# The second feed-forward product of nine blocks as seven quadrant products, with the weight sums formed on chip

## The chip, the cores and the metric

The kernel runs on one core of one Trainium2 chip. The metric is the time of one execution on the device in microseconds (us). Before the change three runs took 1843.79 to 1845.49 us, with a median of 1844.52 us.

## The reference

Two layers of a graph transformer over 2708 nodes with 512 features. All arithmetic is f32. Each layer does this (the adjacency has about 9 neighbours in a row, so a node attends to few others):

```python
q, k, v = h @ Wq.T + bq, h @ Wk.T + bk, h @ Wv.T + bv      # 8 heads of 64
attn = softmax(where(mask == 0, -1e9, q @ k.T / 8))
h1 = layer_norm(h + attn @ v @ Wo.T + bo)
ff = relu(h1 @ W1.T + b1) @ W2.T + b2                      # 512 -> 2048 -> 512
h2 = layer_norm(h1 + ff)
```

The change is in the product with `W2`, in layer 0 alone.

## The kernel before, in words

The kernel turns the adjacency into a list of neighbours for each node, sorts the nodes by the length of their lists into 22 tiles of 128 nodes, and gathers only the listed rows of keys and values. It takes the tiles in 11 blocks of two tiles each (`blocks`, L1581); the last block has a tile of 20 nodes, so its two tiles make 148 columns instead of 256.

The order of the work is written by hand on every engine: each engine runs its instructions in the order in which the program emits them, and an engine that waits holds back all that stands behind it. The order comes from interleaved generators. For each block the main loop (L1753 to L1825) steps through `feed_forward` (L1447), which yields sixteen times, once for each chunk f of 128 of the 2048 hidden features. Between two yields the loop emits other work:

- **The feed-forward itself, on TensorE.** Step f does four matmuls `pf` (L1494) with `W1` as the stationary operand and the 256 columns of the two tiles moving. ScalarE applies the bias and relu and writes `ft` (L1505), 128 features by 256 nodes. Three steps later (`LAG`), `second` (L1460, matmul at L1467) multiplies: for each of the two tiles, `ft` of that tile is stationary, and a 128 by 512 piece of `W2` moves, into the accumulators `a0` and `a1`. After step 15 the last three steps of each tile follow, first of tile one, then of tile two.
- **The end of a block, on VectorE.** L1536 adds the accumulator to the residual; `norm` (L1253) does the layer norm, with a power on GpSimd (L1263) in its middle.
- **The attention of later blocks, on VectorE, ScalarE and GpSimd** (`attend`, L1586). Its steps handle one chunk of up to two neighbours for each node of a tile. VectorE multiplies keys by queries (L1136), sums over heads (L1142), and for the chunk of the step before weighs the values (L1168) and adds them up (L1175 or L1183). ScalarE does the exponentials (L1155) and the scaling of the second neighbour's values (L1162). GpSimd issues the gathers (L1099), three chunks ahead. `advance` (L1645) gives the attention a share of steps after each f, by the table `PACE` (L55): in layer 0 the share is 0.6 after f = 2 to 4, 1.2 after 5 to 8, 0.6 after 9 and 10, 0.8 after 13 to 15, and none after 0, 1, 11 and 12. The first block has its own table `PACES`.
- **The next layer's keys and values** (`keys_values`, L1544): at f = 5 the block before is transposed, at f = 6 and f = 7 its two tiles are multiplied by `Wk` and `Wv`, with VectorE reading the keys out of the accumulator (L1561) and ScalarE the values (L1564). At f = 8 GpSimd puts the rows into DRAM.
- **The next block's input** (`attended`, L1414): at f = 10 and 11 the attended rows are transposed, and at f = 11 multiplied by `Wo`; VectorE adds the residual and norms (L1429 on). At f = 15 the result is transposed again into `hT` (`turned`, L1438).

ps_a, ps_f and ps are the pools of accumulators (one bank of 2 KB a partition for each tile); before, ps_f and ps have three places each. While layer 0 attends, the gathered rows use five places of their own and the place of `Wq`, whose use in layer 0 is over (L1218). SP's queue carries stores and loads: in these blocks the stores of L1566 and L1567.

Of the kernel before, what the change touches and what calls it, by code (L numbers as in the profile page):

```python
# [8 lines left out]
F32 = mybir.dt.float32  # L9
# [14 lines left out]
NC = DM // P  # L24
NP = NH // 2
NFC = FF // P
# [14 lines left out]
KVB = 5  # L41
# [439 lines left out]
def by_edges(ctx: ExitStack, tc: tile.TileContext, x, xT, adj, layers, out, redo):  # L481
# [9 lines left out]
    nc = tc.nc  # L491
# [3 lines left out]
    NL = len(layers)  # L495
# [11 lines left out]
    dram = ctx.enter_context(tc.tile_pool(name="dram", bufs=1, space=DRAM))  # L507
# [5 lines left out]
    ps_f = ctx.enter_context(tc.tile_pool(name="ps_f", bufs=3, space=PSUM))  # L513
    ps = ctx.enter_context(tc.tile_pool(name="ps", bufs=3, space=PSUM))

    own = {}
    all_lines = []
    all_made = []
# [21 lines left out]
    q_d = [dram.tile([N, DM], F32, name=f"q_d{n}") for n in range(NL)]  # L540
    zT_d = [None] + [dram.tile([NT, P, NC, P], F32, name=f"zT_d{n}") for n in range(1, NL)]
    xb_d = [None] + [dram.tile([N, DM], F32, name=f"xb_d{n}") for n in range(1, NL)]
    rec_d = dram.tile([P * NT, 2 * LIST], F32, name="rec_d")

    def chunked(ap):
        return ap.rearrange("(c p) n -> p c n", p=P)
# [578 lines left out]
    class Tile:  # L1125
# [53 lines left out]
        def sums(self, peak):  # L1179
            r, g, S, acc, wide = self.r, self.g, CAPS[self.g], self.acc, self.wide  # L1180
            while wide > 1:
                h = wide // 2
                nc.vector.tensor_tensor(  # L1183
                    acc[:r, :h, :], acc[:r, :h, :], acc[:r, wide - h : wide, :], ALU.add
                )
                wide -= h
            nc.vector.tensor_reduce(
                peak[:r, g : g + 1],
                self.sc[:r, :S, :].rearrange("p s h -> p (s h)"),
                AX.X,  # L1190
                ALU.max,
                apply_absolute_value=True,
            )
# [20 lines left out]
    def rows_of_keys(n):  # L1214

        if n == NL - 1 and not places:
            places.extend([None] * KVB + ["wk", "wv"])
        elif n < NL - 1 and all_made and not places:  # L1218
            places.extend([None] * KVB + ["wq"])
        tag = places[0] if places else None  # L1220
        if places:
            places.append(places.pop(0))
        if tag is None:
            return at.tile([P, SLOTS, 2 * DM], F32, tag="kv", name="kv", bufs=KVB)
        kv = wts.tile([P, NC, DM], F32, tag=tag, name="kv")
        return kv.rearrange("p c n -> p (c n)").rearrange("p (s n) -> p s n", s=SLOTS)
# [55 lines left out]
    class Layer:  # L1282
# [164 lines left out]
        def feed_forward(self, block, hs, hT):  # L1447
# [93 lines left out]
                zs.append(z)  # L1541
            yield zs

        def keys_values(self, block, zs):  # L1544
# [160 lines left out]
    for n in range(NL):  # L1705
# [47 lines left out]
        for k, block in enumerate(blocks):  # L1753
# [5 lines left out]
            for f, zs in enumerate(now.feed_forward(block, hs, hT)):  # L1759
                if f == NFC:  # L1760
                    break
                if f in (5, 6, 7, 8) and behind:
# [19 lines left out]
                    now.load_w2(len(now.w2), nc.scalar)  # L1782
                if n > 0 and (k, f) == (0, 2):
                    now.load_second(1, temp)
                if last and not more and f == 8:
                    checked()
                if last and not more and f == 10:
# [104 lines left out]
```

## Time and profile before

| what | us |
|---|---|
| three runs, lowest, median, highest | 1843.79, 1844.52, 1845.49 |
| the profiled execution's own time | 1844.31 |
| its span | 1842.3 |
| TensorE busy in the span | 1827.5 (99%) |
| VectorE busy in the span | 1374.4 (75%) |
| the nine changed blocks, from the first `pf` of block 1 to the first `pf` of block 10 | 313.23 to 1016.53 |

The profile is of one execution. PE is TensorE's matmul stream, PEld its weight loads, DVE is VectorE, ACT is ScalarE, POOL is GpSimd, SP is SyncE. One matmul of the program in f32 shows as two records, so step f's four `pf` matmuls show as eight. A record's duration overlaps with the next one's. How long a stream takes is therefore read from where records start, not from their mean length.

### The profile page before, as it was taken

To read this page: it belongs to the slowest core of one execution; us is meant where nothing else is said; L and a number is where in the kernel's file an instruction comes from. 1 tells how busy PE (TensorE), PEld (TensorE's weight loads), DVE (VectorE), ACT (ScalarE), POOL (GpSimd) and SP (SyncE) were. 2 spreads that over 40 slices of the span, in tenths; PEclk is the share of its full clock that TensorE was granted. 3 is DMA by queue.
4 is the path that set the end of the run, shared out by engine and by line. 5 is a ranking of instruction groups with operands and counts; after the bars stand their busy time and mean duration, and the time that the engine had idled before them with its cause. 6 is when DMAs were issued, how large, how long until landed. Compare 5 with 4: busy or idle time off the path is not lost.

```text
span 1842.3 us, 20976 instructions
## 1 busy us (share of the span) xinstructions
PE 1827.5 (99%) x6195; PEld 1092.6 (59%) x6195; DVE 1374.4 (75%) x2147; ACT 945.0 (51%) x3263; POOL 782.2 (42%) x745
## 2 busy tenths in 40 slices
PE   9999999999999999999999999999999999999997
PEld 4444466565666656566565544666666666666666
DVE  4986778787777776767774157877998988898853
ACT  4770445554456545555543113655665675567531
POOL 3334755544435434443431032444563645455302
PEclk9999999999999999999999999999999999999999
DMA  9997987644546455553631676845564654555300
GB/s 339 377 340 257 372 273 243 226 158 165 204 139 234 144 187 183 177 182 105 223 121 46 229 264 250 299 132 205 177 225 147 245 206 177 183 197 207 118 12 21
DMA packets 129829, 368.01 MB, mean 200 GB/s; under 512 B 14378, under 2 KB 32670, under 8 KB 129704
## 3 DMA queue, kind: packets, MB, share of 16 engines
q0 software_dynamic: 70608, 252.12, 39.7%
q1 hardware_dynamic: 48938, 92.85, 14.1%
q10 hardware_dynamic: 10158, 21.61, 3.1%
q8 instruction: 50, 0.82, 0.2%
q14 instruction: 75, 0.61, 0.1%
HBM read 315.84 MB, written 50.68 MB: 199 GB/s over the span
## 4 chain that ended last, share of the span: by engine, by line
PE 93%; DVE 3%; ACT 1%; DMA 1%; issue 1%; POOL 0%; SPq 0%; ACTq 0%; POOLq 0%; DVEq 0%
PE pf L1494 30%; PE a L1467 29%; PE o L606 8%; PE v L606 8%; PE k L606 8%; PE q L606 8%; PE tp L1273 3%; DVE sc L1142 1%; DVE kv L1136 1%; ACT kv L1162 1%; PE a L1482 0%; DMA zT<-zT_d 0%; DMA w<-in_W 0%; DMA q<-q_d,ident_i 0%; ACT cx L1206 0%
## 5 line engine op out<-in xcount | busy, mean ns | idle before, releaser
L1494 PE MATMUL pf<-hT,w 128*128 128x256 f32 (+1 forms) x2816 | 631.3, 371 | 0.1
L1494 PEld LDWEIGHTS pf<-hT,w 128*128 128x128 f32 x2816 | 517.7, 190 | 172.6 <-issue 107.0
L1099 POOL DMA_INDIRECT kv<-kv_d,listed x420 | 506.9, 1207 | 253.1 <-issue 113.3
L1467 PE MATMUL a<-w,ft 128*128 128x512 f32 x1312 | 611.1, 592 | 0.0
L1505 ACT ACTIVATE ft<-pf,b 128x256 f32<-128x256 f32 (+1 forms) x336 | 153.9, 461 | 412.0 <-PE pf L1494 402.1
L1467 PEld LDWEIGHTS a<-w,ft 128*128 128x128 f32 x1312 | 246.8, 190 | 187.4 <-issue 165.9
L1263 POOL TENSOR_TENSOR rd<-va,mhalf 128x1 f32<-128x1 f32 (+1 forms) x88 | 81.2, 922 | 564.7 <-DVE va L1261 564.6
L1162 ACT ACTIVATE kv<-kv,p 128x64 f32<-128x64 f32 x1232 | 311.0, 334 | 5.0
L1136 DVE TENSOR_TENSOR kv<-kv,q 128x1024 f32<-128x1024 f32 (+1 forms) x222 | 256.8, 1157 | 14.9 <-DMA q<-q_d,ident_i 13.4
L1142 DVE TENSOR_REDUCE sc<-kv 128x16 f32<-128x1024 f32 (+1 forms) x222 | 257.9, 1162 | 7.6
L1175 DVE TENSOR_TENSOR acc<-acc,kv 128x1024 f32<-128x1024 f32 (+2 forms) x178 | 205.2, 1153 | 76.6 <-ACT kv L1162 60.5
L1155 ACT ACTIVATE p<-sc,listed 128x8 f32<-128x8 f32 x420 | 104.3, 299 | 123.1 <-DVE sc L1142 100.5
L1168 DVE TENSOR_TENSOR kv<-kv,p 128x512 f32<-128x512 f32 (+1 forms) x178 | 123.1, 691 | 36.2 <-ACT p L1155 31.1
L606 PE MATMUL o<-wo,cT 128*128 128x512 f32 x336 | 148.2, 594 | 0.6 <-ACT cT L1278 0.6
L606 PEld LDWEIGHTS o<-wo,cT 128*128 128x128 f32 x336 | 62.2, 190 | 72.5 <-issue 61.7
L731 DVE MAX8 tops<-code 128x8 f32<-128x247 f32 (+2 forms) x242 | 78.7, 399 | 27.1 <-ACT code L726 26.7
L1267 DVE SCALAR_TENSOR_TENSOR h<-h,rd,ln_b 128x512 f32<-128x512 f32 (+1 forms) x88 | 66.1, 751 | 41.0 <-POOL rd L1263 41.0
L1206 ACT ACTIVATE cx<-acc,su 128x64 f32<-128x64 f32 (+1 forms) x352 | 88.2, 332 | 12.9 <-DVE su L1198 7.5
L1162 ACT ACTIVATE acc<-kv,p 128x64 f32<-128x64 f32 (+1 forms) x352 | 88.8, 334 | 1.4
L726 ACT ACTIVATE code<-aj 128x1354 bf16<-128x1354 int32 (+1 forms) x44 | 73.6, 1723 | 21.9 <-POOL aj L720 18.2
L1564 ACT COPY kvs<-v 128x512 f32<-128x512 f32 (+1 forms) x22 | 12.9, 585 | 137.3 <-PE v L606 136.6
L1429 DVE TENSOR_TENSOR h<-o,xb 128x512 f32<-128x512 f32 (+1 forms) x44 | 30.2, 687 | 65.6 <-PE o L606 48.4
(183 smaller groups left out, 1601.7 us busy)
## 6 DMA issues: line engine op xcount, KB each, us to landing
aj<-in_adj SPq DMA_DIRECT2D x42, 677.0 KB
kv_d<-kvs ACTq DMA_DIRECT2D x21, 512.0 KB
xg<-in_xT SPq DMA_DIRECT2D x19, 512.0 KB
w<-in_W SPq DMA_DIRECT2D x16, 512.0 KB
kv<-kv_d,listed POOLq DMA_INDIRECT x420
zT_d<-zT SPq DMA_DIRECT2D x22, 256.0 KB
xb_d<-h SPq DMA_DIRECT2D x21, 256.0 KB
q<-q_d SPq DMA_DIRECT2D x21, 256.0 KB
```

The costliest lines, as they stand in the source:

```text
L606: nc.tensor.matmul(o[:r], xs(c), wm[:, c, :], start=(c == 0), stop=(c == NC - 1))
L1099: return nc.gpsimd.indirect_dma_start(out=to, out_offset=None, in_=table[:, :], in_offset=bass.IndirectOffsetOnAxis(ap=s, axis=0), bounds_ ...
L1136: nc.vector.tensor_tensor(kv[:r, :c, :DM], kv[:r, :c, :DM], self.q[:r].unsqueeze(1).to_broadcast([r, c, DM]), ALU.mult,)
L1142: nc.vector.tensor_reduce(self.sc[:r, s0 : s0 + c, :], kv[:r, :c, :DM].rearrange("p s (h d) -> p s h d", d=DK), AX.X, ALU.add,)
L1155: nc.scalar.activation(p[:r, s, :], self.sc[:r, s, :], AF.Exp, bias=minus[:r, g, s : s + 1])
L1162: nc.scalar.activation(to[:, i, hd], kv[:r, i, DM + h * DK : DM + (h + 1) * DK], AF.Copy, scale=p[:r, s0 + i, h : h + 1],)
L1168: nc.vector.tensor_tensor(to[:, 0, :].rearrange("p (h d) -> p h d", d=DK), kv[:r, 0, DM:].rearrange("p (h d) -> p h d", d=DK), p[:r, s0, : ...
L1175: nc.vector.tensor_tensor(self.acc[:r, :c, :], self.acc[:r, :c, :], kv[:r, :c, DM:], ALU.add)
L1206: nc.scalar.activation(cx[:r, hd], self.acc[:r, 0, hd], AF.Copy, scale=self.su[:r, h : h + 1])
L1467: nc.tensor.matmul(a[:r, cols], fts[f][:, c0 : c0 + r], self.w2[f // 2][:, f % 2, cols], start=(f == 0), stop=(f == NFC - 1),)
L1494: nc.tensor.matmul(pf[:, :w], self.w1[f // 2][:, c, f % 2 * P : f % 2 * P + P], hT[:, c, :w], start=(c == 0), stop=(c == NC - 1),)
L1505: nc.scalar.activation(ft[:, :w], pf[:, :w], AF.Relu, bias=self.b1[:, f : f + 1])
```

## The change

Blocks 1 to 9 of layer 0 (k = 1 to 9, both tiles full) no longer do four matmuls of 512 columns for each pair of chunks f = 2j and 2j + 1. For the first seven pairs they do seven matmuls of 256 columns each (`products`). The left operands are quadrants of the two `ft` tiles and three combinations of them, `s[0]` to `s[2]`; the right operands are quadrants of `W2` and three combinations of them, `t2` to `t4`. One quadrant of `W2` is overwritten by a difference. The eighth pair is done as before, with the second tile's matmuls split into halves.

- VectorE forms the left combinations: `sums` emits four operations of 128 by 128 for each pair. One of them overwrites the second half of an `ft` tile. They are emitted after step f = 2j + 2; the products follow at f = 2j + 3.
- The right combinations are formed by VectorE in block 0 (`form`, four operations of 128 by 256 for each of seven pairs, six of them at f = 5, 7, ... 15 and the seventh at the start of block 1), stored to DRAM on SP's queue, and read back for every pair of every block into five slots (`ask_forms`), three loads of 128 KB for a pair. The slots and the left combinations lie in the place of `Wq`, so the gathers have five places instead of six.
- There are two accumulators more (`c0`, `c1`). ps_f and ps have two places instead of three in blocks 1 to 9.
- At the end of a block nine operations on VectorE put the four accumulators together, in place of two.
- In block 9 the overwritten quadrants of `W2` are loaded again.

```diff
@@ rows_of_keys
-        elif n < NL - 1 and all_made and not places:
-            places.extend([None] * KVB + ["wq"])
@@ class Layer
+        def form(self, j):
+            w, W = self.w2[j], 2 * P
+            b11, b12, b21, b22 = w[:, 0, :W], w[:, 0, W:], w[:, 1, :W], w[:, 1, W:]
+            t2, t3, t4 = (self.slots[(3 * j + i) % 5] for i in range(3))
+            nc.vector.tensor_tensor(t3, b22, b12, ALU.subtract)
+            nc.vector.tensor_tensor(b12, b12, b11, ALU.subtract)
+            nc.vector.tensor_tensor(t2, b22, b12, ALU.subtract)
+            nc.vector.tensor_tensor(t4, b21, t2, ALU.subtract)
+            for i, t in enumerate((t2, t3, t4)):
+                nc.sync.dma_start(out=form_d[j, i], in_=t)
...
+        def ask_forms(self, upto):
+            while self.asked < upto:
+                n = self.asked
+                j, i = n // 3 % (NFC // 2 - 1), n % 3
+                nc.sync.dma_start(out=self.slots[n % 5], in_=form_d[j, i])
+                self.asked += 1
...
+        def feed_forward_by_seven(self, k, block, hs, hT):
...
+            def sums(j):
+                f0, f1 = fts[2 * j], fts[2 * j + 1]
+                s = self.sums[j % 2]
+                nc.vector.tensor_tensor(s[:, 0], f1[:, P:], f0[:, P:], ALU.add)
+                nc.vector.tensor_tensor(f0[:, P:], f0[:, :P], f0[:, P:], ALU.subtract)
+                nc.vector.tensor_tensor(s[:, 1], s[:, 0], f0[:, :P], ALU.subtract)
+                nc.vector.tensor_tensor(s[:, 2], f1[:, :P], s[:, 1], ALU.subtract)
+
+            def products(j):
+                f0, f1, w, s = fts[2 * j], fts[2 * j + 1], self.w2[j], self.sums[j % 2]
+                t2, t3, t4 = (self.slots[(base + 3 * j + i) % 5] for i in range(3))
+                first, last = j == 0, j == J - 1
+                for to, left, right, start, stop in (
+                    (c0[:, L], f0[:, :P], w[:, 0, L], first, False),
+                    (a0[:, L], f1[:, :P], w[:, 1, L], first, False),
+                    (a1[:, L], f1[:, P:], t4, first, False),
+                    (c0[:, R], s[:, 1], t2, False, last),
+                    (c1[:, L], f0[:, P:], t3, first, False),
+                    (c1[:, R], s[:, 0], w[:, 0, R], False, last),
+                    (a0[:, R], s[:, 2], w[:, 1, R], False, False),
+                ):
+                    nc.tensor.matmul(to, left, right, start=start, stop=stop)
...
+                if f % 2 == 0 and j > 0:
+                    sums(j - 1)
+                if f % 2 and j > 0:
+                    products(j - 1)
+                    self.ask_forms(base + min(3 * j + 5, 3 * J + 5 * (k < NB - 2)))
+                    if k == NB - 2:
+                        self.form_back(j - 1)
+                yield None
...
+            nc.vector.tensor_copy(u2, c0[:, L])
+            nc.vector.tensor_tensor(zA[:, L], u2, zA[:, L], ALU.add)
+            nc.vector.tensor_tensor(u2, c0[:, R], u2, ALU.add)
+            nc.vector.tensor_tensor(pair(u34), pair(c1), twice(u2), ALU.add)
+            nc.vector.tensor_tensor(zB[:, R], c1[:, R], zB[:, R], ALU.add)
+            nc.vector.tensor_tensor(zA, a0, zA, ALU.add)
+            nc.vector.tensor_tensor(zB, a1, zB, ALU.add)
+            nc.vector.tensor_tensor(zA[:, R], u34[:, R], zA[:, R], ALU.add)
+            nc.vector.tensor_tensor(pair(zB), pair(zB), twice(u34[:, L]), ALU.add)
+            for z in hs:
+                norm(z, P, self.g2, self.e2)
```

More of the change, by code (lines that the diff above doesn't have):

```diff
@@ L512, in by_edges, with places_of_psum @@
     ps_a = ctx.enter_context(tc.tile_pool(name="ps_a", bufs=1, space=PSUM))
-    ps_f = ctx.enter_context(tc.tile_pool(name="ps_f", bufs=3, space=PSUM))
-    ps = ctx.enter_context(tc.tile_pool(name="ps", bufs=3, space=PSUM))
+    stage = ctx.enter_context(ExitStack())
+    ps_f = ps = ps_s = None
+    def places_of_psum(n, more=False):
+        nonlocal ps_f, ps, ps_s
+        stage.close()
+        ps_f = stage.enter_context(tc.tile_pool(name="ps_f", bufs=n, space=PSUM))
+        ps = stage.enter_context(tc.tile_pool(name="ps", bufs=n, space=PSUM))
+        if more:
+            ps_s = stage.enter_context(tc.tile_pool(name="ps_s", bufs=1, space=PSUM))
+    places_of_psum(3)
     own = {}
@@ L542, in by_edges @@
     xb_d = [None] + [dram.tile([N, DM], F32, name=f"xb_d{n}") for n in range(1, NL)]
+    form_d = dram.tile([NFC // 2 - 1, 3, P, 2 * P], F32, name="form_d")
     rec_d = dram.tile([P * NT, 2 * LIST], F32, name="rec_d")
@@ L1542, in feed_forward, with prepared @@
             yield zs
+        def prepared(self):
+            place = wts.tile([P, NC, DM], F32, tag="wq", name="forms")
+            place = place.rearrange("p c n -> p (c n)")
+            W = 2 * P
+            self.slots = [place[:, i * W : (i + 1) * W] for i in range(5)]
+            sums = place[:, 5 * W :].rearrange("p (two s t) -> p two s t", two=2, t=P)
+            self.sums = [sums[:, i] for i in range(2)]
+            self.asked = 0
+        def form(self, j):
[8 more added lines that the diff above has]
+                nc.sync.dma_start(out=form_d[j, i], in_=t)
@@ new lines, in form_back, with twice, pair @@
+        def form_back(self, j):
+            W = 2 * P
+            nc.sync.dma_start(
+                out=self.w2[j][:, 0, W:], in_=chunked(self.w["W2"])[:, 2 * j, W:]
+            )
+        def ask_forms(self, upto):
[5 more added lines that the diff above has]
+        def feed_forward_by_seven(self, k, block, hs, hT):
+            J, W = NFC // 2 - 1, 2 * P
+            L, R = slice(0, W), slice(W, DM)
+            a0, a1 = (ps_a.tile([P, DM], F32, tag=f"a{i}", name=f"a{i}") for i in range(2))
+            c0, c1 = (ps_s.tile([P, DM], F32, tag=f"c{i}", name=f"c{i}") for i in range(2))
+            fts = []
+            base = 3 * J * (k - 1)
+            def sums(j):
[19 more added lines that the diff above has]
+                    nc.tensor.matmul(to, left, right, start=start, stop=stop)
+            self.ask_forms(base + 5)
+            for f in range(NFC):
+                j = f // 2
+                pf = ps_f.tile([P, DM], F32, tag="f", name="pf")
+                for c in range(NC):
+                    nc.tensor.matmul(
+                        pf[:, :W],
+                        self.w1[j][:, c, f % 2 * P : f % 2 * P + P],
+                        hT[:, c, :],
+                        start=(c == 0),
+                        stop=(c == NC - 1),
+                    )
+                ft = dn.tile([P, W], F32, tag="ft", name="ft", bufs=4)
+                nc.scalar.activation(ft, pf[:, :W], AF.Relu, bias=self.b1[:, f : f + 1])
+                fts.append(ft)
+                if f % 2 == 0 and j > 0:
[6 more added lines that the diff above has]
+                yield None
+            for i in range(2):
+                f, w = 2 * J + i, self.w2[J]
+                nc.tensor.matmul(a0, fts[f][:, :P], w[:, i, :], start=False, stop=i == 1)
+            for cols in (L, R):
+                for i in range(2):
+                    f, w = 2 * J + i, self.w2[J]
+                    nc.tensor.matmul(
+                        a1[:, cols],
+                        fts[f][:, P:],
+                        w[:, i, cols],
+                        start=False,
+                        stop=(cols is R and i == 1),
+                    )
+            zA, zB = hs
+            u2 = dn.tile([P, W], F32, tag="ft", name="u2", bufs=4)
+            u34 = dn.tile([P, DM], F32, tag="row", name="u34", bufs=3)
+            def twice(t):
+                return t.unsqueeze(1).to_broadcast([P, 2, W])
+            def pair(t):
+                return t.rearrange("p (two n) -> p two n", two=2)
+            nc.vector.tensor_copy(u2, c0[:, L])
[9 more added lines that the diff above has]
+                norm(z, P, self.g2, self.e2)
+            yield list(hs)
@@ L1758, in by_edges @@
                 asking = now.queries(blocks[k + AHEAD])
-            for f, zs in enumerate(now.feed_forward(block, hs, hT)):
+            seven = n == 0 and 0 < k < NB - 1
+            if n == 0 and k == 0:
+                now.prepared()
+            if n == 0 and k in (1, NB - 1):
+                places_of_psum(2 + (k > 1), k == 1)
+                if k == 1:
+                    now.form(NFC // 2 - 2)
+            if seven:
+                working = now.feed_forward_by_seven(k, block, hs, hT)
+            else:
+                working = now.feed_forward(block, hs, hT)
+            for f, zs in enumerate(working):
                 if f == NFC:
@@ L1784, in by_edges @@
                     now.load_second(1, temp)
+                if n == 0 and k == 0 and f > 4 and f % 2:
+                    now.form(f // 2 - 2)
                 if last and not more and f == 8:
```

## The prediction

> **What bounds the kernel now.** I read first the page's busy shares, then the changed blocks window by window, then operations kept apart by shape, then one block (k = 3) in order of time.
>
> ```profile
> PE 1827.5 (99%) x6195; PEld 1092.6 (59%) x6195; DVE 1374.4 (75%) x2147; ACT 945.0 (51%) x3263; POOL 782.2 (42%) x745
> ```
>
> TensorE is busy throughout. In windows from one block's first pf to the next's (length; busy time of PE, PEld, DVE, ACT, POOL; clock; DMA):
>
> ```profile
> 470.34:548.67 78.33, 78.33 (x265) 48.04 (x264) 58.11 (x79) 40.37 (x150) 33.97 (x30) 1.00 0.52 175
> ```
>
> Blocks 1 to 8 take 78.3 to 78.8 us each with TensorE never idle and VectorE 55.7 to 61.7 us busy; block 9, when the attention is nearly done, has VectorE at 44.5. So a block now costs its matmuls, and VectorE has about 20 us to spare, but in an order written by hand.
>
> By shape (busy, mean ns of one, idle before):
>
> ```profile
> L1467 PE MATMUL a<-w,ft 128*128 128x512 f32 x1312 | 611.1, 592 | 0.0
> ...
> L1494 PE MATMUL pf<-hT,w 128*128 128x256 f32 x2560 | 595.7, 379 | 0.1
> ...
> L769 DVE TENSOR_TENSOR before<-before,hot 128x48 f32<-128x48 f32 x10 | 2.1, 207 | 0.3
> ```
>
> Block 3 in time order (start, length, and in brackets the idle time before and its releaser):
>
> ```profile
> 469.18 0.64 DVE L1536 TENSOR_TENSOR h<-a,h 128x512 f32<-128x512 f32 x1
> 469.86 0.69 DVE L1257 BATCH_NORM_STATS2 st<-h 128x6 f32<-128x512 f32 x1
> ...
> 476.32 1.22 DVE L1136 TENSOR_TENSOR kv<-kv,q 128x1024 f32<-128x1024 f32 x1
> ...
> 525.65 0.69 DVE L1429 TENSOR_TENSOR h<-o,xb 128x512 f32<-128x512 f32 x1 [4.78 <-PE o L606]
> ...
> 534.30 0.68 DVE L1136 TENSOR_TENSOR kv<-kv,q 128x512 f32<-128x512 f32 x1
> ...
> 545.69 0.69 DVE L1168 TENSOR_TENSOR acc<-kv,p 128x512 f32<-128x512 f32 x1 [1.17 <-ACT p L1155]
> ...
> 547.51 0.64 DVE L1536 TENSOR_TENSOR h<-a,h 128x512 f32<-128x512 f32 x1
> ```
>
> ```profile
> 470.36 7.07 PE L1494 MATMUL pf<-hT,w 128*128 128x256 f32 x32
> 477.27 1.88 PE L1467 MATMUL a<-w,ft 128*128 128x512 f32 x4
> ```
>
> Read the distances: VectorE needs 2.88 us to norm a tile after its addition (469.86 to the second addition at 472.74), 4.32 for a full attention step (476.32 to the next step at 480.64), 8.65 for the next block's two input norms (525.65 to 534.30).
>
> **What it removes.** 32 pf records start 6.91 us apart (470.36 to 477.27), so 0.216 a record, 0.432 a matmul of 256 columns; four records of 512 take 1.72, so 0.86 a matmul. The means (592, 379) overlap and mislead. A pair costs 4 x 0.86 = 3.43 before, 7 x 0.432 = 3.02 after: 0.41 less, 63 times, 25.7 us. Each of the seven stationary loads takes 190 ns, under 216. A block's matmuls would take 75.5.
>
> **What it adds on VectorE.** No row adds 128 or 256 columns from SBUF; between 207 ns (48 columns) and 687 (512, L1429) I interpolate 0.29 and 0.42. Ends: 0.21 and 0.69 each. `sums`: about 1.1 us with its dependent starts, 0.8 to its third operation; seven make 7.7. The nine closing operations: 4.6 (4.2 if none waits for another, 6.5 if all cost 0.72) against 1.3. Together 11 us a block, so 58 becomes 69 busy of 75.5. It fits by sum; the order decides. `form`: 1.7 each.
>
> **The new wait.** Before, TensorE needed VectorE only to free accumulators and for the input norms. Now the fourth product of each pair waits for the third operation of `sums`, which stands on VectorE behind all attention steps emitted earlier. The changed kernel's order on VectorE, block by block, is: nine closings, two norms, sums 0, step, sums 1, two steps, sums 2, keys, two steps, keys, step, sums 3, two steps, sums 4, input norms, sums 5, two short steps, sums 6, a last step, closings. While TensorE waits there, its later matmuls for keys, `o` and `hT` wait too, and these hold VectorE and ScalarE. So I follow the loop around one block, each term from block 3's rows:
>
> 1. VectorE: closings 4.6, two norms 5.8, sums 0 to its third 0.8: 11.2. TensorE reaches that product 8.2 us into the block (6.91 + 3 x 0.432), so it stands.
> 2. TensorE from there to the second tile's values: rest of products 0, 1.7; two f steps 3.45; products 1, 3.0; transposes 0.9; f step 1.7; keys and values 6.9; f step 1.7; products 2, 3.0; keys and values 6.9: 29.3. VectorE's share beside it, about 28, is covered.
> 3. ScalarE then copies the values, does the exponentials, scales: 3.1 (it stands behind that copy in its order).
> 4. VectorE: addition 1.2, sums 3 1.1, two steps 8.6, sums 4 to its third 0.8: 11.7. TensorE needs only 9 here and stands.
> 5. TensorE: rest of products 4, a transpose, the first `o`: 1.7 + 0.4 + 3.4 = 5.6. VectorE idles; before it idled 4.78 at the same place.
> 6. VectorE: input norms 8.65, sums 5 1.1, two short steps 3.2 and 3.7, sums 6 to its third 0.8: 17.4.
> 7. TensorE 1.7; then transposes, ScalarE's copies to `hT` and the exponentials behind them, 3.0 (the transposes before started at 542.66, the operation they hold at 545.69): 4.7.
> 8. VectorE: the tail of the step, 1.8 (545.69 to 547.51), then the next closings.
>
> Sum 11.2 + 29.3 + 3.1 + 11.7 + 5.6 + 17.4 + 4.7 + 1.8 = 84.8, against 78.3: 6.5 us more a block. Block 3's VectorE load (58.1) is near the mean of blocks 1 to 8 (58.5), so eight blocks cost 52. **Ends:** the seventeen `sums` operations on this loop could take 0.6 less or 7.5 more, the closings 0.4 less or 1.9 more; and if every wait on ScalarE in the loop went, VectorE's own work plus item 5 and the norms' pauses would be the floor, 69 + 5.6 + 1.8 + about 1.5 of gaps = 78. So 78 to 94 a block. I take 84.8.
>
> **Block 0.** Four `form`s (6.8) stand before the input norms. VectorE was through its steps at 294.9 and waited till 297.1; now it starts at 301.7, ends at 310.4, and the second transpose, due at 307.7, is 2.7 late. Two more forms, steps, norms and the seventh form put sums 0 of block 1 at about 332.2, where block 1 before would be at 321.5: 10.7 late. From there eight rounds of 84.8 end at 1010.6, in block 9 at the same point where the kernel before stood at 948.5: 62 late. In block 9 the remaining six pairs give back 2.5, and the input norms in item 6 (8.65 + 0.8 against 8.2 of matmuls beside them), with what attention is left, take about the same. I carry 62.
>
> **Other edits.** The loads add 2.75 MB a block to a DMA share of 0.52; SP's stores L1566 and L1567 now stand behind loads that wait for TensorE, and nothing needs them before layer 1 but their buffers. Five gather places: the lead falls from three steps to two (8.6 us) around `kvs`. GpSimd waits more, and its power for the norms stands behind those gathers. Accumulators ps_f at two: `pf` waits for the relu two steps back, with 4.75 us of cover where there was 8.6; ScalarE, 40 us busy, has it. I cost these at nothing; rival C prices them.
>
> **A rule against the change.** The granted clock is 1.00 through every block, but the last window shows 0.50:
>
> ```profile
> 1833.00:1838.00 5.00, 0.46 (x3) 0.05 (x1) 2.62 (x6) 0.00 (x0) 1.94 (x2) 0.99 0.03 7
> 1838.00:1842.30 4.30, 0.00 (x0) 0.00 (x0) 0.00 (x0) 0.00 (x0) 0.04 (x1) 0.50 0.18 67
> ```
>
> The last matmul ended about 1833.5, so some 4.5 us of idleness halved it. What half rate costs, the start of the run shows:
>
> ```profile
> 1.58 3.35 PE L527 MATMUL pr<-ones 128*128 128x128 f32 x14 [1.58 <-POOL ones L524]
> ```
>
> Later records of this width start 0.109 apart, so 14 would take 1.5: a cold start loses 1.8 us. My longest steady stall is item 1's: the closings start about 0.8 after the next block's first pf, 0.8 + 11.2 - 8.2 = 3.8 us. Block 1's is 7 or more. By the rows only block 1 loses its clock, 1.8 us, inside the range. The Trainium skill, "TensorE: Matmul & The Clock Gate" (What's actually happening), says that an idle window of about 3.4 us halves the clock, and a busy one restores it; no run here shows that length. By an estimate from that page a stall of 3.8 would sometimes qualify, each time costing about 1.7 us.
>
> **Rivals.**
> - **A, forecast:** the loop above, 1844.3 + 62 = 1906; 1875 to 1935 with step costs varying from block to block. The profiled 1844.31 is within 0.2 of the median.
> - **B, the products are hidden (faster).** If each `sums` lands before its fourth product, 25.7 us go and block 0 gives 2.7 back: 1821. For it: VectorE idles 20 us a block. Against: that idleness is the waits of items 3, 5 and 7, which stay. It decides where item 1's VectorE stretch falls under 8.2 and item 4's under 9.
> - **C, transfers.** The load for the third product may start only when the pair before has passed its fourth: 5.6 us ahead. The chain of waits has transfers of 4.7 to 7.3 us (larger ones). At 1.7 late, in three uncovered pairs of eight blocks, 41 more: 1947. The seven-place squeeze on gathers works the same way.
> - **D, the clock:** one drop in each of eight blocks at 1.8 us, 14 more: 1920.
> - **E, the floor:** 78 a block, block 0's 10.7 alone: 1845 to 1858.
> - **F, no saving on TensorE:** if seven short matmuls ran by their means (379 and 592), a pair would cost 5.31 against 4.74, and 63 pairs 36 us more than before even with VectorE hidden: 1883. The start distances speak against it.
>
> **Chances.** A 0.66, B 0.08, C 0.09, D 0.08, E 0.08, F 0.01. The likeliest is A, 1906. The range 1858 to 1950 takes in A, C, D and part of E, and leaves out B, a part of E, and dear `sums`. A difference within 0.2% (3.7 us) can hardly be told from none: B gives faster 0.08, E's low edge 0.04 same, the rest slower 0.88.
>
> **What would show it.** In the profile after: windows of blocks 1 to 8 of about 85 us with TensorE busy near 75.5, and its idle time before the products' line put down to VectorE's `sums`, longest at pair 0 (about 4 us) and next at 4, 5 and 6; VectorE near 69 busy, its largest wait still for `o`; block 9 about as long as before; block 0 some 3 longer. I am wrong if the windows are 75 to 77 (B), if the products wait for DMA (C), if the clock row falls (D), or if products start more than 0.216 apart a record (F).

## The result and the profile after

| | before | after |
|---|---|---|
| median of 4 runs each, us | 1845.01 | 1950.69 |
| lowest and highest, us | 1843.79, 1845.79 | 1946.65, 1952.45 |
| the profiled execution, us | 1844.31 | 1950.16 |
| its span, us | 1842.3 | 1948.4 |

The change makes the kernel slower: the ratio is 1.057, with a 95% interval of 1.0557 to 1.0583. The forecast was 1906 with a range of 1858 to 1950. The sign and more than half of the loss were as forecast, and the size was too small by 44.7 us, which puts the median just above the range.

The busy line of the page after (busy time, share of the span, instructions of each engine):

```profile
PE 1842.5 (95%) x6609; PEld 1190.4 (61%) x6609; DVE 1475.6 (76%) x2490; ACT 946.1 (49%) x3263; POOL 793.6 (41%) x745
```

TensorE was busy 1827.5 us before. In 63 pairs it has seven matmuls of 256 columns in place of four of 512, and still it is busy *longer*. That is the first sign that the matmuls themselves became slower somewhere.

The windows of block 1, block 4 (a steady one) and block 9 after, each from its first `pf` to the next block's (length; busy time of PE, PEld, DVE, ACT, POOL; granted clock; DMA share; GB/s):

```profile
318.67:415.81 97.14, 79.73 (x315) 58.56 (x314) 72.74 (x119) 42.76 (x162) 41.02 (x34) 0.91 0.62 199
...
592.99:679.91 86.92, 79.31 (x312) 58.41 (x311) 68.52 (x112) 42.24 (x160) 38.01 (x32) 0.96 0.58 189
...
1031.51:1122.99 91.48, 80.48 (x312) 59.34 (x311) 55.86 (x101) 31.20 (x114) 14.18 (x12) 0.93 0.28 91
```

Two things are to be read. TensorE's busy time is 7.6 us short of block 4's length, so it waits. And its granted clock (the number before the last two) is 0.96 where every block before had 1.00. The clock is either 1.00 or 0.50 at any moment in these traces, so part of the busy time is matmuls at half rate.

Where it waits, by shape and by the view of waits (engine, operation and line, what ended the wait: us in total, times, longest):

```profile
L1619 PE MATMUL c<-forms 128*128 128x256 f32 x126 | 45.4, 445 | 68.1 <-DVE forms L1603 68.1
```

```profile
PE c L1619 <- DVE forms L1603: 68.1, 32, 4.9
```

All 68.1 us of this shape stand before the fourth product of a pair, and all are put down to the third operation of `sums`. Of TensorE's 88.4 us of idleness in blocks 1 to 9 they are the greatest part; 14.8 more are one wait in block 1 (see e4). Block 4 in order of time, TensorE around pair 0:

```profile
592.97 7.07 PE L1626 MATMUL pf<-hT,w 128*128 128x256 f32 x32
599.88 0.59 PE L1619 MATMUL c<-w,ft 128*128 128x256 f32 x2
600.31 0.59 PE L1619 MATMUL a<-w,ft 128*128 128x256 f32 x2
600.74 0.59 PE L1619 MATMUL a<-forms,ft 128*128 128x256 f32 x2
604.59 1.22 PE L1619 MATMUL c<-forms 128*128 128x256 f32 x2 [3.26 <-DVE forms L1603]
605.60 1.06 PE L1619 MATMUL c<-forms,ft 128*128 128x256 f32 x2
606.46 1.06 PE L1619 MATMUL c<-w,forms 128*128 128x256 f32 x2
```

and VectorE beside it:

```profile
593.51 0.37 DVE L1667 COPY u<-c 128x256 f32<-128x256 f32 x1
...
603.73 0.28 DVE L1601 TENSOR_TENSOR forms<-ft 128x128 f32<-128x128 f32 x1
604.04 0.29 DVE L1602 TENSOR_TENSOR ft<-ft 128x128 f32<-128x128 f32 x1
604.25 0.28 DVE L1603 TENSOR_TENSOR forms<-forms,ft 128x128 f32<-128x128 f32 x1
...
657.74 0.69 DVE L1438 TENSOR_TENSOR h<-o,xb 128x512 f32<-128x512 f32 x1 [5.63 <-PE o L617]
```

Products that do not wait start 0.43 apart (599.88, 600.31, 600.74). Behind the gap of 3.26 us they start 0.86 apart (605.60, 606.46): half rate. The same stretch cut into equal pieces of 3.41 us, with the cuts laid where the clock changes, shows how that comes about (length, PE busy, clock, DMA share, GB/s):

```profile
596.59:600.00 3.41, 3.41 (x17) 1.00 0.00 0
600.00:603.41 3.41, 1.33 (x7) 1.00 0.00 0
603.41:606.83 3.42, 2.24 (x5) 0.50 0.38 96
606.83:610.24 3.41, 3.41 (x9) 0.50 0.82 258
610.24:613.65 3.41, 3.41 (x17) 1.00 0.80 241
```

From 250 us on the clock changes only at such cuts, in every trace of this case: the times between two changes are multiples of 3.413 us. Below, the cuts of a trace are called its grid. The piece from 600.00 is idle for 2.1 us, and the next runs at half rate; that one has 1.2 us idle, and the next is at half rate again; that one is full, and full rate comes back.

Blocks by their lengths, from one first `pf` to the next, and the time at half rate in blocks 0 to 9, for all kernels that the text below compares:

| kernel | time, us | block 0 | block 1 | blocks 2 to 8, mean | block 9 | half rate, us |
|---|---|---|---|---|---|---|
| before | 1844.3 | 64.1 | 78.8 | 78.3 | 76.2 | 0 |
| after | 1950.2 | 69.5 | 97.1 | 88.0 | 91.5 | 78.5 |
| e1, sums not read | 1868.6 | 69.0 | 94.0 | 78.5 | 79.5 | 34.1 |
| e2, gap of pair 0 filled | 1939.4 | 69.5 | 101.2 | 86.0 | 89.9 | 44.4 |
| e4, no loads | 1940.2 | 69.5 | 90.1 | 87.6 | 90.9 | 75.1 |
| e5, products a pair later | 1902.7 | 71.9 | 94.9 | 82.8 | 80.3 | 51.2 |
| e6, norms behind sums 0 | 1930.5 | 71.8 | 96.0 | 85.5 | 87.6 | 47.8 |
| e7, sums a step earlier | 1903.6 | 69.8 | 93.8 | 82.7 | 84.8 | 61.4 |
| e9, sums earlier and norms late | 1868.8 | 69.8 | 93.9 | 78.4 | 79.8 | 30.7 |
| e10, e9 from block 2 on | 1848.6 | 64.0 | 78.8 | 78.4 | 79.9 | 10.2 |
| e12, e10 with queries asked earlier | 1840.4 | 64.0 | 78.8 | 77.7 | 78.0 | 0 |

The times in this table are those of the profiled execution; e1 to e9 and e11 ran once each. The kernel before, run beside the experiments, took 1843.6 to 1846.3.

### The profile page after: what moved, and what is told of

Same layout as the page of the kernel before. It is cut to its first block, busy times and chain, and to the rows that moved or that the text cites. A ratio compares the mean times of both kernels' runs of the same rounds, so it can differ in the third digit from the quotient of the medians.

```text
span 1948.4 us, 22649 instructions
## 1 busy us (share of the span) xinstructions
PE 1842.5 (95%) x6609; PEld 1190.4 (61%) x6609; DVE 1475.6 (76%) x2490; ACT 946.1 (49%) x3263; POOL 793.6 (41%) x745
## 4 chain that ended last, share of the span: by engine, by line
PE 43%; DVE 4%; ACT 2%; issue 1%; POOL 1%; DMA 0%; POOLq 0%; DVEq 0%
PE pf L1503 15%; PE a L1476 14%; PE o L617 4%; PE q L617 3%; PE tp L1282 1%; PE pf L1626 1%; PE c L1619 1%; PE k L617 1%; PE v L617 1%; ACT kv L1173 1%; DVE sc L1153 1%; DVE kv L1147 1%; PE a L1619 1%; POOL rd L1272 1%; PE a L1491 0%
## 5 line engine op out<-in xcount | busy, mean ns | idle before, releaser
L1110 POOL DMA_INDIRECT kv<-kv_d,listed x420 | 517.4, 1232 | 363.3 <-issue 113.4
L1503 PE MATMUL pf<-hT,w 128*128 128x256 f32 (+1 forms) x1664 | 365.0, 367 | 3.4 <-ACT ft L1514 3.3
L1503 PEld LDWEIGHTS pf<-hT,w 128*128 128x128 f32 x1664 | 301.3, 191 | 104.8 <-issue 63.0
L1476 PE MATMUL a<-w,ft 128*128 128x512 f32 x736 | 343.4, 592 | 0.0
L1626 PE MATMUL pf<-hT,w 128*128 128x256 f32 x1152 | 272.4, 390 | 4.9 <-ACT ft L1634 4.9
L1147 DVE TENSOR_TENSOR kv<-kv,q 128x1024 f32<-128x1024 f32 (+1 forms) x222 | 257.2, 1159 | 18.6 <-DMA q<-q_d,ident_i 14.8
L1626 PEld LDWEIGHTS pf<-hT,w 128*128 128x128 f32 x1152 | 225.9, 197 | 50.2 <-issue 13.4
L1476 PEld LDWEIGHTS a<-w,ft 128*128 128x128 f32 x736 | 138.2, 190 | 104.0 <-issue 92.2
L1514 ACT ACTIVATE ft<-pf,b 128x256 f32<-128x256 f32 (+1 forms) x192 | 87.6, 459 | 227.6 <-PE pf L1503 216.8
L1634 ACT ACTIVATE ft<-pf,b 128x256 f32<-128x256 f32 x144 | 66.7, 465 | 248.4 <-PE pf L1626 204.5
L1619 PE MATMUL c<-forms 128*128 128x256 f32 x126 | 45.4, 445 | 68.1 <-DVE forms L1603 68.1
```

What stands on the lines that cost most here:

```text
L1110: return nc.gpsimd.indirect_dma_start(out=to, out_offset=None, in_=table[:, :], in_offset=bass.IndirectOffsetOnAxis(ap=s, axis=0), bounds_ ...
L1147: nc.vector.tensor_tensor(kv[:r, :c, :DM], kv[:r, :c, :DM], self.q[:r].unsqueeze(1).to_broadcast([r, c, DM]), ALU.mult,)
L1476: nc.tensor.matmul(a[:r, cols], fts[f][:, c0 : c0 + r], self.w2[f // 2][:, f % 2, cols], start=(f == 0), stop=(f == NFC - 1),)
L1503: nc.tensor.matmul(pf[:, :w], self.w1[f // 2][:, c, f % 2 * P : f % 2 * P + P], hT[:, c, :w], start=(c == 0), stop=(c == NC - 1),)
L1626: nc.tensor.matmul(pf[:, :W], self.w1[j][:, c, f % 2 * P : f % 2 * P + P], hT[:, c, :], start=(c == 0), stop=(c == NC - 1),)
```

## The experiments

**Theory 1:** TensorE loses its time where the fourth product of a pair waits for `sums`, by the wait and by the half rate behind it. **Rivals:** the loads of the right combinations; the smaller edits (five gather places, two accumulators); VectorE's added work as such, wherever it stands; short matmuls that are slower by themselves.

### e1: the products read plain quadrants

```diff
-                nc.vector.tensor_tensor(f0[:, P:], f0[:, :P], f0[:, P:], ALU.subtract)
+                nc.vector.tensor_tensor(s[:, 1], f0[:, :P], f0[:, P:], ALU.subtract)
...
-                    (c0[:, R], s[:, 1], t2, False, last),
+                    (c0[:, R], f1[:, P:], t2, False, last),
...
-                    (c1[:, R], s[:, 0], w[:, 0, R], False, last),
-                    (a0[:, R], s[:, 2], w[:, 1, R], False, False),
+                    (c1[:, R], f0[:, :P], w[:, 0, R], False, last),
+                    (a0[:, R], f1[:, :P], w[:, 1, R], False, False),
```

> The four operations of sums stay on VectorE, but write only to the scratch place, and the products read plain quadrants of ft in place of the sums, so no product waits for VectorE (what is computed is no longer the reference's). Theory 1, the products' wait for VectorE is the loss, with the half-rate stretches that follow its stalls: blocks 1 to 9 fall from 86-92 us to 75-79, TensorE's idle before the products goes, the clock stays at 1.00 after block 1, and the time is 1825 to 1860. Rival, VectorE's added work or the gathers' lost place are the loss: blocks stay above 84, time above 1915.

Measured: 1868.63. A steady block:

```profile
567.89:643.57 75.68, 75.68 (x311) 56.69 (x310) 67.45 (x112) 42.58 (x160) 37.85 (x31) 1.00 0.68 222
```

TensorE never idles in it at full clock, with VectorE as loaded as in the changed kernel (67.5 us). So in a steady block the seven matmuls do save what they should, VectorE's work costs nothing by itself, and the dependence costs some 82 of the 106 us. What is left stands in blocks 0, 1, 8 and 9, which are 4.9, 15.2, 7.2 and 3.3 us longer than in the kernel before. By these it came out 9 us above the upper end that theory 1 gave, and the clock did not stay at 1.00 behind block 1: 13.7 us at half rate are left in blocks 6, 8 and 9.

### e2: matmuls that fill the gap of pair 0

```diff
                     nc.tensor.matmul(to, left, right, start=start, stop=stop)
+                    if first and right is t4:
+                        for _ in range(8):
+                            nc.tensor.matmul(c1[:, L], left, w[:, 1, L], start=True, stop=True)
```

> Eight matmuls of 256 columns (3.5 us), whose result is never used, run before the fourth product of pair 0 of each block, in the stall of 3.3 to 4.9 us. Theory 1 with the clock as a cost of its own: the half-rate stretch after pair 0 goes, 2.5 to 3.5 us in each of blocks 2 to 9, the stalls at pairs 3, 4 and 5 stay; time 1920 to 1932. Rival, VectorE sets the pace and the slow matmuls lie beside it: 1945 to 1952.

Measured: 1939.39, between what theory 1 gave and what the rival gave. More work on TensorE makes the kernel 11 us *faster*. Blocks 2 to 9 got 15.3 us shorter with 34 us less at half rate; block 1 got 4 longer, because there the matmuls come behind a third product that is itself late. The waits for `sums`, 68.1 us without these matmuls, became:

```profile
PE c L1619 <- DVE forms L1603: 40.6, 28, 3.1
```

So the clock is a cost of its own, and its size can be estimated. The 72 matmuls are 31.1 us of work at full rate. TensorE's idleness in blocks 1 to 9 fell by 26.5 us (88.4 to 61.8), all of it at pair 0; elsewhere it stayed at 57. By that alone the kernel would be 4.6 us slower. It is 10.8 faster, so 34 us less at half rate gave back some 15 us, nearly half of their length.

### e3: the smaller edits alone

```diff
@@ the kernel before, in part
-        elif n < NL - 1 and all_made and not places:
-            places.extend([None] * KVB + ["wq"])
...
+            if n == 0 and k in (1, NB - 1):
+                places_of_psum(2 + (k > 1))
```

> The kernel before with two of the changed kernel's side edits alone: five gather places instead of six, and two places in ps_f and ps in blocks 1 to 9. Theory 1 counts them at nothing: 1843 to 1850. Rival, they are a part of the loss: 1855 to 1890.

Measured: 1845.56, beside 1844.30 for the kernel before. One run of each: they cost nothing that can be told.

### e4: no loads of the right combinations

```diff
...
-                nc.sync.dma_start(out=self.slots[n % 5], in_=form_d[j, i])
...
-                t2, t3, t4 = (self.slots[(base + 3 * j + i) % 5] for i in range(3))
+                t2, t3, t4 = w[:, 1, R], w[:, 1, L], w[:, 0, L]
```

> No right-hand form is loaded back; the products read quadrants of W2 in place of the slots (what is computed is no longer the reference's). Forms are still made and stored. Theory 1: only block 1's long stall (14.8 us, where the first loads come after the last form's store) shrinks, to about 8: time 1938 to 1944. Rival, loads that come late cost in every block: under 1925.

Measured: 1940.23. Block 1 is 7.1 us shorter and block 8 2.7; the others are as they were within 0.6. The loads cost one round trip, at block 1's pair 0; no run shows what shortens block 8. In block 1 of the changed kernel SP's queue and TensorE show the round trip:

```profile
338.31 2.49 SPq L1586 DMA_DIRECT2D forms<-form_d  x5
```

```profile
341.82 1.19 PE L1619 MATMUL a<-forms,ft 128*128 128x256 f32 x2 [14.77 <-DVE kv L1147]
```

The first loads stand behind the stores of the seventh form, and the third product behind the loads. The releaser named is not the one that ended this wait: the operands are `forms` and `ft`, the same product in e9 is put down to `DMA forms<-form_d`, 15.2 us, and in e4, without the loads, it waits 2.6.

### e5: the products a pair later

```diff
-            self.slots = [place[:, i * W : (i + 1) * W] for i in range(5)]
+            self.slots = [place[:, i * W : (i + 1) * W] for i in range(3)]
+            self.extra = [place[:, i * W : (i + 1) * W] for i in (3, 4)]
...
-                if f % 2 and j > 0:
-                    products(j - 1)
+                if f % 2 and j > 1:
+                    products(j - 2)
...
+            products(J - 1)
...
```

> The changed kernel with the seven products of a pair issued one pair later (two steps of f more between sums and products; the last pair's behind step 15), ft in six places instead of four, and three slots for the loaded forms instead of five to make room. No work is left out or added. Theory 1 (each block loses 7 to 11 us of TensorE's time because the products stand directly behind sums that VectorE gives late, and 3 to 6 us more because those gaps drop TensorE's clock): with 6 to 7 us more between them the gaps close and the clock holds; blocks 2 to 9 take 76 to 80 us instead of 86 to 92, 1835 to 1875 us. Rival (VectorE's own queue is too long for a block, so that any distance is used up within a block or two): blocks stay over 83 us, over 1905 us.

Measured: 1902.74, above theory 1's range and just under the rival's. No wait for `sums` is left among TensorE's waits; others have taken its place:

```profile
PE a L1620 <- DMA forms<-form_d: 32.6, 11, 10.3
PE pf L1627 <- ACT ft L1637: 17.4, 8, 4.9
```

Three slots were too few, so loads now came late, and the relu stood behind ScalarE's share of the attention. The run says that distance removes the wait for `sums`; it does not say what that is worth.

### e6 and e7: two ways to give the sums earlier

```diff
@@ e6: the output norms of blocks 1 to 8, behind sums 0 of the next block
                 if f % 2 == 0 and j > 0:
                     sums(j - 1)
+                    if j == 1:
+                        self.end_norms()
...
@@ e7: sums one step earlier
-                if f % 2 == 0 and j > 0:
-                    sums(j - 1)
+                if f % 2 and j < J:
+                    sums(j)
```

> The changed kernel with the two output norms of blocks 1 to 8 (5.8 us of VectorE) emitted behind sums 0 of the next block instead of ahead of them. No work is left out. Theory 1: the wait of 3.3 us at pair 0 goes, and with it the clock drop behind it (about 3 us a block); about 2 us of wait comes up at pair 1, too short for a drop; blocks 2 to 8 take 82 to 85 us, 1915 to 1930 us. Rival (the loop through VectorE is closed, the same wait stands at the next pair): 1940 to 1955 us, blocks as before within 1.5 us.

Measured: 1930.53. The wait at pair 0 is gone in blocks 2 to 9. At pair 1 now stand 2.2 us in blocks 3, 4, 6 and 7, as expected, and 3.2 to 3.8 in blocks 2, 5, 8 and 9; some 2.55 us at pair 4 stay in most steady blocks. Half rate fell from 78.5 to 47.8 us and did not go. The time is half a microsecond above theory 1's range, and three of blocks 2 to 8 are above its 85 us.

> The changed kernel with the sums of a pair emitted one step earlier, right behind the relu of its second half and ahead of that step's attention (and, for pair 5, ahead of the input norms' wait for the product with Wo). No work is left out. Theory 1: the waits at pairs 3, 4 and 5 (0.4, 2.6 and 1.4 us a block in the steady blocks) go, pair 0 keeps its 3.3 us and its clock drop; 3.5 to 4.5 us a block, 1908 to 1925 us. Rival (what is gained there comes back as a longer wait at pair 0, since VectorE ends its block no earlier): 1940 to 1955 us.

Measured: 1903.59, a little better than expected: the waits at pairs 3, 4 and 5 are gone, and pair 0 keeps 3.2 to 4.9 us.

### e9: both, with one norm behind sums 0 and one behind sums 1

```diff
+                if f % 2 and j < J:
+                    sums(j)
+                    if self.late:
+                        norm(self.late.pop(0), P, self.g2, self.e2)
...
```

> The changed kernel with the sums one step earlier and, in blocks 1 to 8, the output norms late: that of tile one behind sums 0 of the next block, that of tile two behind its sums 1. No work is left out. Theory 1: with sums 0 straight behind the closings the wait at pair 0 falls under 1 us, none of over 2 us is left in blocks 3 to 7, and these take 76 to 79 us; blocks 0 and 1 stay near 70 and 92; 1860 to 1880 us. Rival (VectorE's queue is the loop and a wait must stand somewhere): blocks 3 to 7 at 81 to 83 us as with the earlier sums alone, 1890 to 1905 us.

Measured: 1868.8, in theory 1's range. Blocks 3, 4 and 7 take 75.9 to 76.0 and block 5 77.4; block 6, with a wait of 2.0 us for a relu and a drop of the clock behind it, takes 79.9, above the 79 expected. Block 4 has about as much VectorE work as in the changed kernel (68.5):

```profile
568.88:644.88 76.00, 75.67 (x311) 56.76 (x310) 67.64 (x112) 42.59 (x160) 39.02 (x31) 1.00 0.67 219
```

So the same work in another order is 81 us faster, as fast as e1 without the dependence. The rival that VectorE's work must cost, wherever it stands, falls for the steady blocks; blocks 0 and 1 still take 69.8 and 93.9.

### e10 and e12: block 1 ordinary, queries earlier

```diff
@@ e10: the right combinations are formed in block 1, without the overwritten quadrant
             nc.vector.tensor_tensor(t3, b22, b12, ALU.subtract)
-            nc.vector.tensor_tensor(b12, b12, b11, ALU.subtract)
-            nc.vector.tensor_tensor(t2, b22, b12, ALU.subtract)
+            nc.vector.tensor_tensor(t2, t3, b11, ALU.add)
...
-            seven = n == 0 and 0 < k < NB - 1
+            seven = n == 0 and 1 < k < NB - 1
...
+                if n == 0 and k == 1 and f % 2 and f < NFC - 1:
+                    now.form(f // 2)
+                if n == 0 and k == 1 and f > 4 and f % 2:
+                    now.form_in_place(f // 2 - 2)
...
@@ e12: and in attend
+                if n == 0 and q is None and g != order[-1]:
+                    q = asked(n, order[order.index(g) + 1])
                 if k > 0:
                     kv = next(loaded)
@@ and in the main loop
-                advance((PACE if k else PACES)[n][f])
+                advance((PACE if k else PACES)[n][f] + 0.2 * (n == 0 and k == NB - 2 and 4 < f < 9))
```

> The same, and the seven products only in blocks 2 to 9: block 1 stays ordinary and the right combinations are formed in it, three operations of 128 by 256 a pair from f = 1 on and the overwriting one behind the quadrant's last use. No work is left out. Theory 1: block 0 is back at 64, block 1 takes 79 to 84 and block 2 no round trip of 15 us (its third product finds its load done), so eight blocks at 76 to 79 stand against 78.3; 1838 to 1860 us. Rival (the cost is VectorE's added work, wherever it stands): 1875 us or more.

Measured: median 1849.01 of 10 runs, 1844.23 to 1850.61; ratio to the kernel before 1.0021, 1.0011 to 1.0030. Block 0 and block 1 are back at 64.0 and 78.8: forming the combinations in a block that is otherwise done as before costs nothing. Block 8 kept a wait of 4.2 us, where VectorE waited 4.5 for the queries of the next tile:

```profile
DVE kv L1147 <- DMA q<-q_d,ident_i: 4.5, 1, 4.5
```

> The seven products in blocks 2 to 9 as in the run before it (1849.0 us), with two of its three last long gaps addressed: the queries of the next tile in layer 0 are asked for ahead of the next gathers of keys instead of behind them, where they stood behind a wait of 6.5 us for a free place and made VectorE wait 4.5 us in block 8; and block 9's attention gets 0.2 more a step at f = 5 to 8, so that less of it is left for f = 10. No work is left out. Theory (a gap over 2 us costs itself and a clock drop): block 8 falls from 84.3 to 77 to 79, block 9 from 79.9 to 76 to 78, 1839 to 1845 us, level with the kernel before or up to 0.3% faster. Rival (the attention needs that time anyway, and the gap comes back at another step): 1846 us or more.

Measured: median 1844.68 of 11 runs; ratio 0.9999, 0.9990 to 1.0008, so level with the kernel before. Two edits went in together; block 8 came out 0.4 us above what was expected, block 9 within it. Blocks 4, 8 and 9:

```profile
547.64:623.62 75.98, 75.67 (x311) 56.76 (x310) 67.43 (x112) 42.55 (x160) 37.84 (x31) 1.00 0.66 220
856.02:935.41 79.39, 76.21 (x311) 56.70 (x310) 67.49 (x116) 42.45 (x159) 35.04 (x30) 1.00 0.59 196
935.41:1013.40 77.99, 74.19 (x311) 54.88 (x310) 55.69 (x101) 31.64 (x114) 13.91 (x12) 1.00 0.35 111
```

The profiled execution, the fastest of the eleven, took 1840.43 without a piece at half rate, 4 us less than the kernel before. The eleven runs spread over 7.5 us (1840.43 to 1847.90), the kernel before over 2.2. This trace has gaps of 1.9 to 2.05 us in blocks 2, 5, 6 and 9, just at the bound that the next experiment finds, so whether they drop the clock can differ from run to run. The mean granted clock, which is on record for every run, agrees: it is 0.999 in the fastest, never rises as the runs get slower, and is 0.996 in the slowest. So the slower runs had more time at half rate; that these gaps were what dropped the clock is argued, since only one execution has a trace.

### e8 and e11: what a gap costs

```diff
@@ the kernel before, in feed_forward
+                if self.n == 0 and f == 2 and w == 2 * P and block != blocks[0]:
+                    link = small.tile([P, DK], F32, tag="link", name="link", bufs=1)
+                    nc.scalar.copy(link, fts[1][:, :DK])
+                    for _ in range(LINKS[blocks.index(block) - 1]):
+                        nc.scalar.copy(link, link)
+                    nc.tensor.matmul(
+                        pf[:DK, w : w + P], link, self.w1[0][:, 0, :P], start=True, stop=True
+                    )
```

> The kernel before, with one gap put into TensorE's stream in each of blocks 1 to 9: ahead of step 2's first matmul TensorE waits for a chain of 4 to 22 copies on ScalarE (128 by 64, some 0.33 us each), the shortest in block 1, the longest in block 9, and does one small matmul more. So nine gaps of about 1.5 to 8 us measure what a gap costs. Theory 1 (a gap of about 3.3 us or more halves TensorE's clock for 3.4 us or a multiple): blocks with gaps under 3 us are longer by the gap alone, those over 3.5 us by the gap and 1.7 to 3.5 us more, with half rate behind the gap; 1885 to 1900 us in all. Rival (the drops of the changed kernel have another cause than the gap, such as its order of weights or its 256-column products): no half rate behind the gaps, blocks longer by the gaps alone, 1875 to 1885 us.

Measured: 1888.45, in theory 1's range, but not as it had it:

| block | 1 | 2 | 3 | 4 | 5 | 6 | 7 | 8 | 9 |
|---|---|---|---|---|---|---|---|---|---|
| gap, us | 1.67 | 2.22 | 2.50 | 2.77 | 3.05 | 3.32 | 4.15 | 4.98 | 6.64 |
| block longer by, us | 2.3 | 4.4 | 3.1 | 3.4 | 3.7 | 4.0 | 6.5 | 7.5 | 9.8 |
| half rate, us | 0 | 3.4 | 0 | 0 | 0 | 0 | 3.4 | 6.8 | 6.8 |

A gap of 2.22 us dropped the clock and one of 3.32 did not. No bound on a gap's length explains that. The pieces of the grid do. Block 2's gap:

```profile
396.96:400.37 3.41, 1.30 (x7) 1.00 0.00 0
400.37:403.78 3.41, 3.30 (x8) 0.50 0.42 103
```

Block 6's gap:

```profile
724.63:728.05 3.42, 1.55 (x8) 1.00 0.00 0
728.05:731.46 3.41, 1.96 (x9) 1.00 0.32 77
731.46:734.87 3.41, 3.41 (x14) 1.00 0.96 344
```

The short gap lies almost whole in one piece and leaves it 2.1 us idle. The long one is shared, 1.87 and 1.45, and neither piece is idle enough. Cut on their grids, the traces of after and of eleven experiments (all but e3) give this for the piece that follows a piece at full rate, from 250 to 1240 us: after over 2.05 us of idleness, half rate 80 times of 80; after 1.71 to 2.05, 6 times of 25, and what decides there is open; after less, 0 of 3235. A piece at half rate is followed by another when it is idle for 0.62 us or more (54 of 54), and by full rate when for 0.48 or less (86 of 86).

> The kernel before with gaps again, this time of two lengths: chains of 4 copies (1.7 us) in blocks 1, 3, 5, 7 and 9 and of 13 copies (4.15 us) in blocks 2, 4, 6 and 8. Theory, formed from the runs up to here: the clock is set for each piece of a fixed grid of 3.41 us by the piece before, and a piece in which TensorE is idle for over about 2 us halves the next one; then no short gap drops the clock and every long one does, whatever its place on the grid; short blocks 0.6 us over their gap, long ones 2.2 to 3 us over it; 1872 to 1877 us. Rival (a chance drop behind gaps of any length over some 2 us): one or more of the long gaps without a drop, or a short one with one.

Measured: 1884.30. All five short gaps (1.67) left the clock alone, and all four long ones (4.15 to 4.16) dropped it, for 3.4 or 6.8 us. Short ones lengthened their blocks by 2.3 us, long ones by 6.2 to 7.8. A gap of 4.15 must leave at least one piece 2.07 us idle, wherever it lies. The total in the expectation was added up wrongly: five times 2.3 and four times 6.35 to 7.15 make 37 to 40, so 1881 to 1884. The rival, drops by chance, is out for gaps of these two lengths.

## Why the prediction was right about the loop and wrong about the size

The 106.4 us that blocks 0 to 9 gained, split by the windows (idle is the length less TensorE's busy time; the half-rate term is the busy time of blocks 1 to 9, 716.0, less 681.8, which these blocks take at full rate: 605.7 for blocks 2 to 9 in e12, and for block 1 an estimate of 76.1, e9's 78.7 less half of the 5.2 it was busy at half rate). It is a split of the time, not four separate experiments:

| term | forecast | measured |
|---|---|---|
| TensorE's saving | -25.7 | -21.5 |
| TensorE idle, blocks 1 to 9 | about 85 | 88.4 |
| half rate, blocks 1 to 9 | none, or 1.8 | 34.2 |
| block 0 | 2.7 | 5.3 |
| sum | 62 | 106.4 |

The idle forecast is what the carried 62 contains beside the saving and block 0. That its total came out so near is in part luck: 9.3 us a block gives 65 in blocks 2 to 8, where 60.0 were measured, and leaves about 20 for blocks 1 and 9, where 28.4 were.

- **The failed step** is "By the rows only block 1 loses its clock, 1.8 us". The row behind it showed a halved clock after 4.5 us of idleness, and the text took that length as the bound, with its longest steady stall at 3.8. The stalls at pair 0 of blocks 2 to 9 came out at 3.2 to 4.9 us, four of the eight shorter than forecast, and the clock fell at every one; what failed was the bound. About 2 us within one piece of the grid are enough. The row itself fits that: its clock fell at 1837.91, and the whole piece before it, from 1834.50, was idle. So rival D's mechanism acted in every block, beside A and not in place of it, and at 34.2 us in place of its 14: more than one drop in blocks 2, 8 and 9, and two pieces for many a drop. With 34 us in place of none the same working gives 1940, inside the range; the other 10 us are idleness (3.4), block 0 (2.6) and the smaller saving (4.2). By the estimate under e2 time at half rate costs nearly half of its length, which for the 75 us in blocks 1 to 9 agrees with 34.
- The Trainium skill, "TensorE: Matmul & The Clock Gate" (What's actually happening), gives a free-running window of 3413 ns, and an idle window as the condition for half rate. The traces agree on the length (3.413 us) and on its running freely: TensorE's first matmul starts at 1.58 to 1.59 us in every trace, and the first piece at full rate begins anywhere from 4.4 to 7.2. On the condition the measurement decides: a window idle for some 60% was enough. The estimate that the prediction made from that page, "sometimes", at 1.7 us each, was nearer than the row it preferred.
- **The loop, A,** holds. In block 4 item 1 took 11.0 us (593.51 to the end of L1603 at 604.53), forecast 11.2; VectorE's wait for `o` 5.63, forecast 5.6; VectorE busy 68.5, forecast 69. The waits stand where they were expected: longest at pair 0, then 2.6 at pair 4, 1.4 at pair 5. At pair 6 one came in block 3 alone (1.3). Steady blocks lost 7.4 to 8.9 us to idleness; the forecast had 9.3.
- **What it adds on VectorE:** closings 4.5 (forecast 4.6), sums 1.05 (1.1), a form 1.7 (1.7). These prices were right.
- **What it removes:** 0.43 a product at full rate, as forecast. A full-rate block without stalls has TensorE busy for 75.7 to 76.3, forecast 75.5, so the saving was 4.2 less in all.
- **Block 0** lost 5.3 in place of 2.7. The forms delay the attention's reduction, ScalarE's exponentials wait for it, and a relu stands behind them, so `pf` waited 3.3 us and the clock fell. The page has it as the one wait of this line:

```profile
L1503 PE MATMUL pf<-hT,w 128*128 128x256 f32 (+1 forms) x1664 | 365.0, 367 | 3.4 <-ACT ft L1514 3.3
```

- **Block 1** contains the round trip of the forms, 7.1 us by e4, which the text had not put into its sum.
- **Block 9** was to take about as long as before, and took 15.2 more: it has waits for `sums` of 4.9, 2.8 and 3.1 us, each followed by half rate. The text took the attention's end as the end of such waits; closings, norms and what is left of the attention still stand ahead of `sums`.
- **Other edits** at nothing: right, by e3. **C** acted in block 1 (7.1 us), and perhaps in block 8 (2.7 by e4). **B** stated its condition rightly, VectorE's stretch of item 1 under 8.2: where e9 brings it there, blocks take 76.0. **F** is out: products that do not wait start 0.43 apart.

## What to carry to other kernels

Work that moves from a full engine to one with time to spare is free only if its results come in time: follow the in-order queue to each place where the full engine will wait. Where the granted clock falls behind short stalls, they cost more than their length, so add up idleness per piece of the clock's grid and not by the length of a gap. Before giving up such a change, look at what stands ahead of the awaited operations: in the steady blocks two norms that nobody needed yet stood ahead of the worst wait (e6), and reordering alone took the kernel from 5.7% slower to 1.3% (e9).

## What the runs showed of the hardware

- TensorE's clock goes by pieces of 3.413 us that run freely: about 2 us of idleness in a piece halve the next, and it stays halved until a piece has less than about 0.5 us of idleness. In e8 and e11 a gap without a drop lengthens a block by its length and 0.6 us, in which the small matmul of these edits is contained; one with a drop by 2.1 to 3.6 us more than its length.
- The kernels with gaps near 2 us vary more from run to run: e12 spread over 7.5 us and e10 over 6.4, the kernel before over 2.2, and within e12 the granted clock goes from 0.999 in the fastest run to 0.996 in the slowest.
- On VectorE an f32 operation of two tensors took mostly 0.28 to 0.29 us for 128 columns, 0.42 for 256 and 0.69 for 512 in the changed kernel.
